# Queries' cast placed behind the exponentials, x of batch 0 loaded in its own steps, one transpose and one root moved ahead, in a post-norm transformer block on one core

## The chip, the cores and the metric

The kernel runs on one core of one Trainium2 chip. The metric is the device time of one execution in microseconds (us), lower is better. Times of separate runs and one profiled execution are given. All times inside the kernel are counted from the start of the profiled span.

## The reference

Input x has 4 batches of 512 tokens with 512 features, in float32. One block is computed: attention with 16 query heads of 32 and one shared key and value head, rotary position terms on queries and keys, a layer norm, a gated feed-forward with ternary weights, a layer norm.

```python
q = (x @ Wq + bq).reshape(B, T, H, HD).transpose(0, 2, 1, 3)
k = (x @ Wk + bk)[:, None]
v = (x @ Wv + bv)[:, None]
q, k = _rotary(q, HD), _rotary(k, HD)
attn = softmax(q @ k.T / sqrt(HD))
x = _layernorm(x + (attn @ v) @ Wo + bo)
quant = lambda w: clip(round(w / (mean(abs(w)) + 1e-8)), -1, 1)
hidden = sigmoid(x @ quant(w1).T) * (x @ quant(w2).T)
x = _layernorm(x + hidden @ quant(w3).T)
```

## The kernel before, in words

The attention is one list of 64 steps, `(b, c, t)`: 4 batches, 4 chunks `c` of four heads, 4 tiles `t` of 128 keys. A step computes transposed scores for four heads (`ps`, two PSUM tiles of two banks), exponentials on ScalarE (`es`, two instructions of 128x1024), and one step later the weighted values (`acc`). The maximum that softmax subtracts comes from a second product (`pmax`) made `LEAD` = 7 steps ahead and reduced on VectorE (`mx`). `ps` and `pmax` share the two buffers of the PSUM pool `ps_sc`, so a `pmax` waits until `es` has read the bank. In batch 0 the sums of the exponentials are a product (`den` from `es`); in batches 1 to 3 GpSimd adds them up over the four tiles (`total`, four instructions of 128x512 a step), and `den` is one product of `total` at the end of a chunk.

All engines but the DMA engines run their instructions in the order in which the program issues them: `act`, `dve`, `pool`, `mm`, `move` and `transpose` (lines 70 to 86) pin every instruction, so the trace shows L75 for all ScalarE, VectorE and GpSimd work, L80 for products, L83 for SP's transfers and L86 for transposes. The order is made by Python generators:

- `fill` hands out pieces of other work to TensorE between the steps: `project_in` (keys, values, queries of later batches), `project_out` (output product, first norm, transposes `pt`), `feed_forward`. Each `yield` gives the length of a piece.
- `late` is a list of generators with a slot number. `due()` (line 752) raises the slot and advances each one whose slot has come. It is called twice a step: in the middle, and at the end. So a small task such as `store_q` gets one piece of itself issued in each half-step.
- `quantized` is advanced by `quantize`, up to two jobs a step. A job loads one weight tile on GpSimd's queue four jobs ahead (`raw` from `in_wf`), takes its absolute sum (`junk`) or its sign (`sgn`) on ScalarE, finishes it on VectorE and stores it (`w` from `raw`).

`project_in` (line 262) makes one query chunk: product `pq`, then `turn` on VectorE (four instructions: `a`, a shuffle, a product, the addition that writes `q`), and then it enters `store_q` (line 328) in `late` with slot + 1, after the `yield` that follows. `store_q` casts `q` on ScalarE, subtracts on GpSimd to get the tail, and one half-step later stores `q` (`qw`) and head and tail (`qp`) through SP. `load_head` reads `qp` back (`qr`) for the `pmax` products. `load_xT` loads the transposed x of a later batch at the end of `project_in`, on SP's queue.

`normalize` (line 458) turns a chunk's sums into reciprocals through two small transfers (`flat`, `few`), spreads them (`rden`) and multiplies `ctxT` on GpSimd; the last chunk of a batch has fewer idle half-steps in it. `load_x` (line 525) loads four tiles of x of the same batch, and in the next four half-steps adds the output bias `bo_sb` to them on GpSimd; it is entered 6 slots after a batch's last step. `project_out` adds its product to these tiles, so they must be there by then.

After the last step two blocks are left: the rest of batch 2's feed-forward and batch 3's. `bank` (line 226) then hands out banks of `ps_mm` and `ps_sc` in turn. In the last part of a feed-forward, the `while` ahead of the products `po` holds them until enough tiles of the next batch are transposed (`transposed`); `split` copies each transposed tile as a head on ScalarE and a tail on VectorE (`y`). The first product `gu` of the next feed-forward needs all four tiles. At the very end, tiles 0 to 2 of batch 3 are normalized on ScalarE, and the last one by `last_norm` (line 676), half on ScalarE and half on VectorE.

Of the kernel before, what the change touches and what calls it, by code (L numbers as in the profile page):

```python
# [28 lines left out]
def postln_block(  # L29
# [232 lines left out]
    def project_in(b):  # L262

        s = batches[b]
        n = P - HD
        while now < NC * NT * (b - 2):
            yield 0

        pk = ps_mm.tile([P, T], F32, tag="mm", name="pk")
        for c in range(NC):  # L270
            mm(pk, wkv_sb[:, c, :], s.xT[c], c == 0, c == NC - 1)
            if c == 1:
                yield -1.8
        kv = work.tile([P, T], F32, tag="kv", name="kv", bufs=1)
        act.activation(kv[n:P], pk[n:P], AF.Identity, bias=bkv_sb[n:P, 0:1])
        s.kT = work.tile([P, T], F32, tag="kT", name="kT", bufs=3)
        rotation = turn(
            [(s.kT[0:n], slice(0, n)), (s.kT[n:P], slice(0, HD))],
            pk, bkv_sb[:, 0:1], bkv_sb[:, 1:2], n, now < 0,
        )  # L280
        next(rotation)
        yield 1.8
        next(rotation, None)
        if b > 0:
            late.append((slot + 2, split_k(b)))
        for c in range(NC):

            while b + 1 == B and c + 2 >= NC and not batches[0].projected:
                yield 0
            pq = ps_mm.tile([P, T], F32, tag="mm", name="pq")  # L290
            for d in range(NC):
                mm(pq, wq_sb[c][:, d, :], s.xT[d], d == 0, d == NC - 1)
                if d == 1:
                    yield -1.8
            if b == 0:

                if c == 0:
                    room = work.tile([P, NC, T], F32, tag="y0", name="room", bufs=1)
                q = s.q[c] = room[:, c, :]
            else:  # L300
                q = work.tile([P, T], F32, tag="q", name="q")
            rotation = turn(
                [(q, slice(0, P))], pq, bq_sb[:, c : c + 1], bq_sb[:, NC + c : NC + c + 1], P, now < 0
            )
            next(rotation)
            if c == 0:
                pv = ps_mm.tile([P, NT, HD], F32, tag="mm", name="pv")
                for t in range(NT):
                    transpose(pv[:, t, :], kv[n:P, ts(t, P)], ident[n:P, n:P])
                s.v = work.tile([P, NT, HD], F32, tag="v", name="v", bufs=3)  # L310
                act.copy(s.v, pv)
            yield 1.8
            next(rotation, None)
            if b > 0:
                late.append((slot + 1, store_q(b, c, q)))
            s.done = c + 1
        load_xT(NC if b == 0 else 2)
# [140 lines left out]
    def normalize(b, c):  # L458

        s = batches[b]  # L460
        if b > 0:
            s.den = ps_acc.tile([P, T], F32, tag="den", name="den")
            columns(s.den, ones[:, 0:HD], s.total, True, True)

        sums = work.tile([P, T], F32, tag="sums", name="sums", bufs=1)
        act.copy(sums, s.den)
        yield
        flat = [dram.tile([NG, T], F32, tag=f"flat{i}", name="flat", bufs=3) for i in range(2)]
        move(flat[0], sums.rearrange("(i r) k -> i r k", r=HD)[:, 0])
        yield  # L470
        few = small.tile([P, NG * T // P], F32, tag="few", name="few")
        move(few, flat[0].rearrange("i (r j) -> (i r) j", r=HD))
        yield

        if c + 1 < NC:
            yield
        dve.reciprocal(few, few)
        move(flat[1].rearrange("i (r j) -> (i r) j", r=HD), few)
        yield
        rden = work.tile([P, T], F32, tag="rden", name="rden", bufs=1)  # L480
        for i in range(NG):
            move(rden[ts(i, HD), :], flat[1][i].partition_broadcast(HD))
        yield
        if c + 1 < NC:
            yield
        pool.tensor_tensor(s.ctxT[c], s.ctxT[c], rden, ALU.mult)
        yield
# [94 lines left out]
    def feed_forward(b):  # L582
# [32 lines left out]
        for k, fs in enumerate(parts):  # L615
# [21 lines left out]
            ahead = NT // 2 if fs[-1] + 1 == NF else 1  # L637
            for some in [range(ahead)] + [(t,) for t in range(ahead, NT)]:

                while fs[-1] + 1 == NF and b + 1 < B and 0 <= batches[b + 1].transposed <= some[-1]:  # L640
                    yield 0
                pos = {t: bank("po") for t in some}
                last = len(fs) - 1
                early = [(t, n) for t in some for n in range(last)]

                put = len(early) - 1 if b + 1 == B and len(some) > 1 else len(early)
                for t, n in early[:put] + [(some[0], last)] + early[put:] + [(t, last) for t in some[1:]]:
                    for i in range(2):
                        mm(
                            pos[t],  # L650
                            h[n][i][:, ts(t, P)],
                            w3[k][n],
                            n == 0 and i == 0,
                            n == last and i == 1,
                        )
                for t in some:
                    dve.scalar_tensor_tensor(s.x[t], pos[t], 0.5, s.x[t], ALU.mult, ALU.add)
                    if fs[-1] + 1 < NF:
                        continue
                    stats(s.x[t], mv, t)  # L660
                    if b + 1 == B:
                        for done in range(max(t - 1, 0), t if t + 1 < NT else NT):
                            if done + 1 < NT:
                                for _ in layernorm(s.x[done : done + 1], mv[:, done : done + 1, :], True):
                                    pass
                                late.append((slot + 1, store(b, done)))
                            else:
                                last_norm(s.x[done], mv[:, done, :])
                    elif t == NT - 1:
                        late.append((slot + 1, layernorm(s.x, mv)))  # L670
                yield 0.24 * 2 * len(fs) * len(some)
# [1 line left out]
            for t in range(NT):  # L673
                late.append((slot + 6, store(b, t)))

    def last_norm(h, mv):

        y, shift = (small.tile([P, 1], F32, tag=f"end{k}", name="end") for k in range(2))
        act.activation(y, mv[:, 1:2], AF.Sqrt, bias=eps_t)
        dve.reciprocal(y, y)  # L680
        dve.scalar_tensor_tensor(shift, mv[:, 0:1], -1.0, y, ALU.mult, ALU.mult)
        left, right = slice(0, D // 2), slice(D // 2, D)
        act.activation(h[:, left], h[:, left], AF.Identity, bias=shift, scale=y)
        dve.tensor_scalar(h[:, right], h[:, right], y, shift, ALU.mult, ALU.add)
        pin(nc.scalar.dma_start(out=out[B - 1, ts(NT - 1, P), left], in_=h[:, left]))
        move(out[B - 1, ts(NT - 1, P), right], h[:, right])

    def store(b, t):
        move(out[b, ts(t, P), :], batches[b].x[t])
# [53 lines left out]
    PER = NC * NT  # L743
    LEAD = 7
    late = []
    slot = 0

    now = -1
# [3 lines left out]
    def due():  # L752

        nonlocal slot
        slot += 1
        for entry in list(late):
            if slot >= entry[0] and next(entry[1], "end") == "end":
                late.remove(entry)

    def ask(k):  # L760

# [6 lines left out]
    def find_maxima(k, *chunks):  # L768

        if k >= len(steps):  # L770
            return
        b, c, i = steps[k]
        if chunks[0] == 0:
            ask(k + HEADS)
            while batches[b].done <= c or (b and k not in heads):
                if batches[b].done <= c:
                    fill.one()
                else:
                    due()
                    ask(k)  # L780
        if b == 0:
            row_maxima(b, c, i, chunks[0] // 2)
        else:
            maximum(b, c, i, chunks, heads[k])
        if i == NG - 1 and chunks[-1] == NT - 1:

            late.insert(0, (slot + (1 if now < 0 else 2), spread(b, c)))
# [22 lines left out]
    for n, (b, c, t) in enumerate(steps):  # L810
# [7 lines left out]
        if last is not None and last[0] == 0:  # L818
            count(*last)
        last = (b, c, t, es)  # L820
        if t == NT - 1:
            begin = slot + 3
            late.append((begin, normalize(b, c)))
            if c == NC - 1:
                late.append((begin + 7, feed(b)))
                late.append((slot + 6, load_x(b)))
        if batches[-1].done < NC:

            find_maxima(n + LEAD, 0, 1)
            due()  # L830
            find_maxima(n + LEAD, 2, 3)
            quantize(1)
# [2 lines left out]
        else:  # L835
            find_maxima(n + LEAD, 0)
            fill.draw(0.4 * pace)
            find_maxima(n + LEAD, 1, 2)
            due()
            fill.draw(0.3 * pace, True)  # L840
            find_maxima(n + LEAD, 3)
# [72 lines left out]
```

## Time and profile before

| what | us |
|---|---|
| median of 3 runs | 693.89 |
| the runs | 690.67 to 695.45 |
| the profiled execution | 693.86 |
| its span, first to last instruction | 692.1 |
| ScalarE cast of the queries, 128x512 | 0.60 to 0.62 |
| GpSimd: tail of the queries, 128x512 | 1.26 to 1.33 |
| GpSimd: one step's `total`, four instructions | 4.94 to 4.97 |
| GpSimd: bias added to one tile of x | 1.26 to 1.28 |
| ScalarE: one step's `es`, two instructions | 1.93 to 1.94 |

The kernel's steps can be found in the trace by their `ps` products: those of batch 0 end at 154, the four of batch 1's first chunk start at 154.16, 162.32, 174.99 and 183.47. Batch 1's projection ran during batch 0, as did those of batches 2 and 3 in part. The attention ends at about 560; batch 2's last feed-forward products end at 622, and batch 3's feed-forward fills the rest.

A timeline row reads: start, duration, engine, line, operation, output from inputs, shape, number of instructions merged, and in brackets the engine's idle time before it and what ended it. PE is TensorE's product row, PEld its weight loads, DVE is VectorE, ACT ScalarE, POOL GpSimd, SP the queue that issues most transfers.

### The profile page before, as it was taken

The page shows a single profiled execution, that of the slowest core. Times are in us where ns is not written, and L with a number is a line of the kernel's source. Part 1 is how long each engine was busy: PE and PEld are TensorE (multiplying, and loading weights), DVE is VectorE, ACT ScalarE, POOL GpSimd, SP SyncE. Part 2 cuts the span into 40 slices and gives each one's busy share as a digit, 9 for nine tenths or more (in the row PEclk, how much of TensorE's full clock was granted, in tenths as well). Part 3 has the DMA queues.
Part 4 walks back from the last instruction along what each step waited for, and adds up shares of the span by engine and source line. Part 5 has one row for each costly group of instructions (what it writes and reads, how often), then busy time and mean ns, then how long its engine had stood idle before and what let it go on. Part 6 is the DMA issues. An engine that isn't in the chain of part 4 may idle for free.

```text
span 692.1 us, 9555 instructions
## 1 busy us (share of the span) xinstructions
PE 660.5 (95%) x3318; PEld 360.7 (52%) x3318; DVE 392.9 (57%) x570; ACT 290.3 (42%) x454; POOL 324.8 (47%) x414
## 2 busy tenths in 40 slices
PE   8989999998989979999999999999999999999995
PEld 6333333443333345565455565654554676777884
DVE  1887765785756655655555764455434433454435
ACT  2474556653443654434334445243344421234213
POOL 1624432446788684556555373666574803202000
PEclk9999999998999999999999999999999999999999
DMA  8746665787665465345223347341221464235631
GB/s 293 243 165 215 216 203 165 225 262 242 198 208 155 136 222 165 109 148 168 72 61 95 110 135 240 115 159 40 67 85 41 149 219 137 70 113 181 197 110 61
DMA packets 59807, 107.20 MB, mean 155 GB/s; under 512 B 13680, under 2 KB 14448, under 8 KB 59760
## 3 DMA queue, kind: packets, MB, share of 16 engines
q1 hardware_dynamic: 51696, 80.51, 37.6%
q0 software_dynamic: 7920, 25.96, 11.3%
q8 instruction: 26, 0.43, 0.2%
q14 instruction: 21, 0.17, 0.1%
q10 hardware_dynamic: 144, 0.13, 0.1%
HBM read 83.76 MB, written 22.81 MB: 154 GB/s over the span
## 4 chain that ended last, share of the span: by engine, by line
PE 85%; DVE 9%; ACT 3%; issue 1%; DMA 1%; POOL 0%; DVEq 0%; ACTq 0%; POOLq 0%
PE gu L80 24%; PE po L80 18%; PE ps L80 12%; PE pmax L80 9%; PE acc L80 8%; PE pq L80 7%; PE den L80 4%; DVE mx L75 3%; ACT es L75 2%; PE pk L80 2%; DVE xt L75 1%; PE warm L80 1%; DMA xT<-in_xT 1%; DVE y L75 1%; DVE st L75 1%
## 5 line engine op out<-in xcount | busy, mean ns | idle before, releaser
L75 DVE TENSOR_REDUCE mx<-pmax 128x1 f32<-128x512 f32 (+1 forms) x159 | 158.5, 1009 | 107.6 <-PE pmax L80 107.4
L75 ACT ACTIVATE es<-ps 128x1024 f32<-128x1024 f32 x128 | 124.2, 1022 | 126.9 <-PE ps L80 118.9
L80 PE MATMUL gu<-y,wg 128*128 128x512 f32 x704 | 173.7, 396 | 2.5 <-DVE y L75 1.6
L80 PEld LDWEIGHTS gu<-y,wg 128*128 128x128 f32 x704 | 130.9, 188 | 41.9 <-issue 6.9
L75 POOL TENSOR_TENSOR total<-total,es 128x512 f32<-128x512 f32 x96 | 123.6, 1318 | 50.6 <-ACT es L75 50.6
L80 PE MATMUL po<-wd,h 128*128 128x512 f32 x352 | 87.7, 396 | 3.7 <-DVE y L75 2.1
L75 POOL TENSOR_TENSOR total<-es 128x512 f32<-128x512 f32 x48 | 60.2, 1283 | 63.4 <-ACT es L75 63.4
L80 PE MATMUL pmax<-kr,qr 128*128 128x512 f32 x192 | 76.5, 463 | 8.8 <-ACT es L75 8.6
L80 PEld LDWEIGHTS po<-wd,h 128*128 128x128 f32 x352 | 64.7, 188 | 23.6 <-issue 3.4
L75 ACT CAST h<-hw 128x512 fp32r<-128x512 f32 x44 | 27.3, 620 | 97.6 <-DVE hw L75 97.5
L80 PE MATMUL acc<-es,v 128*32 128x512 f32 x512 | 68.2, 605 | 0.0
L80 PEld LDWEIGHTS pmax<-kr,qr 128*128 128x128 f32 x192 | 34.3, 192 | 63.3 <-ACT es L75 26.0
L75 DVE SCALAR_TENSOR_TENSOR hw<-th,gu 128x512 f32<-128x512 f32 x44 | 30.3, 688 | 57.5 <-PE gu L80 54.2
L75 DVE SCALAR_TENSOR_TENSOR xt<-po,xt 128x512 f32<-128x512 f32 x48 | 33.0, 688 | 47.8 <-PE po L80 47.6
L80 PE MATMUL po<-wo_sb,ctxT 128*128 128x512 f32 x128 | 59.1, 594 | 0.3 <-DVE hw L75 0.3
L80 PE MATMUL ps<-negm,ones_r 2*128 2x512 f32 x256 | 57.8, 788 | 0.0
L80 PE MATMUL ps<-qT,kT 32*128 32x512 f32 x384 | 55.2, 640 | 0.0
L75 DVE TENSOR_TENSOR h<-hw,h 128x512 fp32r<-128x512 f32 x44 | 41.3, 938 | 22.6 <-ACT h L75 22.3
L80 PE MATMUL pq<-xT,wq_sb 128*128 128x512 f32 x112 | 53.2, 603 | 1.0 <-ACT v L75 1.0
L75 POOL DMA_DIRECT2D raw<-in_wf x66 | 35.9, 546 | 37.5 <-ACT junk L75 19.3
L75 ACT ACTIVATE th<-gu 128x512 f32<-128x512 f32 x44 | 26.3, 598 | 47.5 <-PE gu L80 47.5
L80 PEld LDWEIGHTS po<-wo_sb,ctxT 128*128 128x128 f32 x128 | 23.9, 189 | 23.5 <-issue 21.1
(98 smaller groups left out, 624.6 us busy)
## 6 DMA issues: line engine op xcount, KB each, us to landing
wg<-w SPq DMA_DIRECT2D x88, 256.0 KB
raw<-in_wf POOLq DMA_DIRECT2D x66, 256.0 KB, 4.3
qr<-qp SPq DMA_DIRECT2D x96, 128.0 KB
wd<-w SPq DMA_DIRECT2D x44, 256.0 KB
w<-raw POOLq DMA_DIRECT2D x33, 256.0 KB, 4.3
qp<-q SPq DMA_DIRECT2D x48, 128.0 KB
rden<-flat SPq DMA_DIRECT2D x64, 64.0 KB
xt<-in_x SPq DMA_DIRECT2D x16, 256.0 KB
```

Of the source, the lines that this page charges most:

```text
L75: return lambda *args, **kw: pin(getattr(self.engine, name)(*args, **kw))
L80: pin(nc.tensor.matmul(out, lhsT=lhsT, rhs=rhs, start=start, stop=stop))
```

## The change

It has four parts.

1. In the main loop `project_in` asks at once whether `turn` is through; if so, `store_q` goes into a new list `middle`. `begin_middle()` moves that list into `late` just before the `due()` in a step's middle, so that the cast comes after that step's `es`.
2. `load_x(0)` is entered in the middle of batch 0 (step 8 of 16) instead of 6 slots after its last step; other batches keep their place.
3. The last chunk of batch 0 gets one more idle half-step in `normalize`, so that its `ctxT` product comes later in GpSimd's order.
4. After the last step, one more tile of the next batch must be transposed before the products `po` of a part's end. And the root of the last tile's norm is issued ahead of the norm of the tile before it; the last tile is normalized by VectorE alone, in two halves, each stored when done.

```diff
+            whole = b > 0 and next(rotation, "end") == "end" if now >= 0 else False
+            if whole:
+                middle.append((slot, store_q(b, c, q)))
             yield 1.8
             next(rotation, None)
-            if b > 0:
+            if b > 0 and not whole:
                 late.append((slot + 1, store_q(b, c, q)))
...
-        if c + 1 < NC:
+        if c + 1 < NC or b == 0:
             yield
         pool.tensor_tensor(s.ctxT[c], s.ctxT[c], rden, ALU.mult)
...
-                while fs[-1] + 1 == NF and b + 1 < B and 0 <= batches[b + 1].transposed <= some[-1]:
+                while fs[-1] + 1 == NF and b + 1 < B and 0 <= batches[b + 1].transposed <= min(
+                    some[-1] + (now == len(steps)), NT - 1
+                ):
                     yield 0
...
-                        for done in range(max(t - 1, 0), t if t + 1 < NT else NT):
-                            if done + 1 < NT:
-                                for _ in layernorm(s.x[done : done + 1], mv[:, done : done + 1, :], True):
-                                    pass
-                                late.append((slot + 1, store(b, done)))
-                            else:
-                                last_norm(s.x[done], mv[:, done, :])
+                        for done in range(max(t - 1, 0), t):
+                            norm = layernorm(s.x[done : done + 1], mv[:, done : done + 1, :], True)
+                            next(norm)
+                            if t + 1 == NT:
+                                end = last_scale(mv[:, t, :])
+                            for _ in norm:
+                                pass
+                            late.append((slot + 1, store(b, done)))
+                        if t + 1 == NT:
+                            last_norm(s.x[t], *end)
...
+    def last_scale(mv):
         y, shift = (small.tile([P, 1], F32, tag=f"end{k}", name="end") for k in range(2))
         act.activation(y, mv[:, 1:2], AF.Sqrt, bias=eps_t)
+        return y, shift, mv
+
+    def last_norm(h, y, shift, mv):
         dve.reciprocal(y, y)
         dve.scalar_tensor_tensor(shift, mv[:, 0:1], -1.0, y, ALU.mult, ALU.mult)
-        left, right = slice(0, D // 2), slice(D // 2, D)
-        act.activation(h[:, left], h[:, left], AF.Identity, bias=shift, scale=y)
-        dve.tensor_scalar(h[:, right], h[:, right], y, shift, ALU.mult, ALU.add)
-        pin(nc.scalar.dma_start(out=out[B - 1, ts(NT - 1, P), left], in_=h[:, left]))
-        move(out[B - 1, ts(NT - 1, P), right], h[:, right])
+        for k, engine in enumerate((nc.scalar, nc.sync)):
+            half = ts(k, D // 2)
+            dve.tensor_scalar(h[:, half], h[:, half], y, shift, ALU.mult, ALU.add)
+            pin(engine.dma_start(out=out[B - 1, ts(NT - 1, P), half], in_=h[:, half]))
...
+    def begin_middle():
+        late.extend(middle)
+        middle.clear()
...
+        if n == NC * NT // 2:
+            late.append((slot, load_x(0)))
         if t == NT - 1:
             begin = slot + 3
             late.append((begin, normalize(b, c)))
             if c == NC - 1:
                 late.append((begin + 7, feed(b)))
-                late.append((slot + 6, load_x(b)))
+                if b > 0:
+                    late.append((slot + 6, load_x(b)))
         if batches[-1].done < NC:
             find_maxima(n + LEAD, 0, 1)
+            begin_middle()
             due()
```

`begin_middle()` stands ahead of the other two calls of `due()` in a step's middle in the same way. In the order of instructions, TensorE's differs only in the place of one group of four transposes; ScalarE's and GpSimd's differ in the places of the casts and their tails, of the four bias additions and of one `ctxT`, and at the end; SP's in the places of `qw`, `qp`, the loads of x, and the `rows`, `qr`, `negm`, `rden` next to them.

## The prediction

> **What bounds the kernel.** I read the page first: its busy times, its slices, its chain.
>
> ```profile
> PE 660.5 (95%) x3318; PEld 360.7 (52%) x3318; DVE 392.9 (57%) x570; ACT 290.3 (42%) x454; POOL 324.8 (47%) x414
> PEclk9999999998999999999999999999999999999999
> ```
>
> TensorE is the bound nearly everywhere: 95% busy, and the chain is 85% PE. So a change pays only where PE stands still or runs slowly: 692.1 - 660.5 = 31.6 us of idle time, and wherever the granted clock is below 1. I then asked who PE waits for, and took the clock over short windows.
>
> ```profile
> PE pmax L80 <- ACT es L75: 9.5, 14, 2.6
> PE gu L80 <- DVE y L75: 1.6, 1, 1.6
> 163.10:166.50 3.40, 1.59 (x16) 1.00 0.82 298
> 166.50:169.90 3.40, 2.75 (x6) 0.50 0.88 251
> 169.90:173.30 3.40, 3.40 (x5) 0.50 0.87 259
> 173.30:176.70 3.40, 3.40 (x20) 0.99 0.64 172
> 190.40:193.80 3.40, 1.25 (x16) 1.00 0.81 242
> 193.80:197.20 3.40, 2.94 (x10) 0.50 0.60 183
> ```
>
> In the first two rows the numbers are us in total, times, longest. The other rows give the stretch, its length, PE's busy time, the granted clock, the DMA share and GB/s. Twice PE is busy for under half of a stretch (1.59 and 1.25 of 3.40 us) and the next one or two run at clock 0.50. So a wait is paid twice. The cause stands in the timeline, first of PE and ScalarE at 162 to 178, then at 189 to 198:
>
> ```profile
> 162.88 0.81 PE L80 MATMUL ps<-negm,ones_r 2*128 2x512 f32 x4
> 165.07 0.62 ACT L75 CAST q<-q 128x512 fp32r<-128x512 f32 x1 [5.74 <-DVE q L75]
> 165.59 1.93 ACT L75 ACTIVATE es<-ps 128x1024 f32<-128x1024 f32 x2
> 166.66 1.22 PE L80 MATMUL pmax<-kr,qr 128*128 128x512 f32 x2 [1.98 <-ACT es L75]
> 169.44 3.78 PE L80 MATMUL pk<-xT,wkv_sb 128*128 128x512 f32 x4 [0.49 <-DMA xT<-in_xT]
> ...
> 192.66 0.62 ACT L75 CAST q<-q 128x512 fp32r<-128x512 f32 x1 [5.22 <-DVE q L75]
> 193.19 1.93 ACT L75 ACTIVATE es<-ps 128x1024 f32<-128x1024 f32 x2
> 194.26 1.22 PE L80 MATMUL pmax<-kr,qr 128*128 128x512 f32 x2 [2.61 <-ACT es L75]
> 195.41 2.21 PE L80 MATMUL den<-total,ones 128*32 128x512 f32 x8
> ```
>
> The scores are ready at 163.69, but the exponentials (`es`) stand on ScalarE behind the queries' cast, and the cast waits for VectorE's `q`. `es` starts at 165.59, and PE's next product needs the bank that `es` reads.
>
> **The cast.** The changed program puts each cast just after the `es` of a step instead of before the next one; PE's order is unchanged there. Elsewhere PE's wait at this place is about 0.17 us.
> - First stall: 1.98 - 0.17 = 1.8 us. Its slow clock: two pairs of `pmax` at 1.22 and 1.20 against 0.73 make 1.0; `pk` at 3.78 against 1.98 makes 1.8; `pm` and the start of `pq` 0.2: together 3.0.
> - Second stall: 2.61 - 0.17 = 2.4. Its slow clock: `pmax` 1.22 against 0.73, `den` 2.21 against 1.07: 1.6.
> - Third place, batch 1 to 2: `pmax` waits 0.54 at 237.22 and 1.87 at 245.67 behind casts at 235.63 and 244.08; less 0.17 each, 2.1. The transposes behind wait 0.71 and 1.18 for VectorE's `y`, which hangs on ScalarE's casts behind the same `es`; I add 0.3. Bounds 1.4 (half of it returns in the transposes) and 3.5.
>
> What is late next? (a) The 0.49 before `pk` is a wait for xT, issued on SP at 163.50 and 5.90 us on the chain. At full clock and without the stall `pk` is due at about 166.5, so xT must be issued by about 160.6. SP held it behind the `qp` store, which waited for GpSimd's `q` (160.37), which stood behind `ctxT` (159.15, 3.77 waiting for its transfer). In the new order this `q` subtraction is two DMA pairs ahead of `ctxT`; its cast follows the `es` that end at 151.3, so it can run at about 152.3, `qp` issues behind `rden` (152.16 to 155.0) at about 156.7, and xT at about 159.6. So the 0.5 goes as well. (b) `den` needs GpSimd's sums: next part.
>
> **GpSimd's row.** Before: four additions of the output's bias (1.26 to 1.28 us each), `ctxT` (1.26) and casts' tails stand among the sums; the third `total` runs 190.97 to 195.92, while `den` starts at 195.41. It hid behind the stalls; with PE some 8 us earlier, `den` is due at about 187. After: from the first `es` (164.6), three `total` (4.94 + 4.97 + 4.95), one `q` 1.26, `kr` 1.28 and six DMA issues of 0.55 make 20.7, ending at 185.3: 1.7 us early. With two bias additions and `ctxT` still in front (3.8) it would be 189.1, 2 us late. So this edit earns nothing alone; it keeps the cast's gain. `ctxT`, one half-step later, then ends at 186.6; `po` wants it at about 189.
> The four loads of x (256 KB) are issued at about 105 instead of 178.24, 1.85 us of SP. Queued behind them on SP: `flat` (ready at 106.8), `qr`, `few`, `rows`, each with steps to spare. The additions wait on GpSimd for landings; the raw loads (`raw`, 103.73 and 110.69) queue behind the first two. A raw load lands in 4.3 to 4.8 us and its reader comes two steps (13 us) later in program order, so some 7 us of delay are hidden; price zero, bounds -0.5 and +3.
> Sum at 155 to 200: 1.8 + 3.0 + 0.5 + 2.4 + 1.6 = 9.3; bounds 5.5 and 10.5.
>
> **Three transposes ahead.** Only where batch 3 follows batch 2 after the attention. The `gu` at 622.01 runs one product and waits 1.59 for the last `y` (623.28 on VectorE), queued behind two pieces of `xt`, `st`, `mv`. In the new order the last transpose precedes the third `po`, and its `y` stands behind two such pieces instead of three, less one `y` moved ahead of them. By VectorE's rows (0.69 `y`, 0.69 `xt`, 0.69 `st`, 0.18 `mv`; about 1.6 a piece overlapped) the last `y` ends near 622.5 instead of 623.9: 1.4. A bank is reused sooner, so the second `po` may wait some 0.4 for the first `y`, which partly replaces the 0.38 at 617.55. I take 1.3, bounds 0.4 and 1.7.
>
> **The end.** Before, ScalarE does the norm of tile 2 (686.63, 0.81), then the root (687.35), and VectorE's two small steps end at 688.02; the halves run side by side to 688.65 and the store is issued at 688.68. After: root at 686.4, small steps end near 687.05, VectorE does both halves in turn (2 x 0.41) to 687.9. ScalarE still normalizes tile 2 until 687.5, then issues the left half; SP issues the right one at 687.9, tile 2 behind it. 688.65 - 687.9 is about 0.7; bounds 0.2 and 1.1.
>
> **Sum.** 9.3 + 2.4 + 1.3 + 0.7 = 13.7. The profiled execution took 693.86 (span 692.1), the median is 693.89, so nothing is to be corrected: 680.2 us. Bounds of the gains, 7.5 and 16.8, give 677.1 to 686.4.
>
> **Rivals.**
> *A: the slow clock stays.* By the trace, 1.8 idle us in one 3.4 us stretch cost the clock, 1.2 idle us (241.6 to 245.0, clock 1.00) did not. New waits of 1 to 2 us in these steps (VectorE is 29.2 of 45 us busy there) would keep the 3.0 + 1.6: 680.2 + 4.6 = 684.8. The Trainium skill, TensorE: Matmul & The Clock Gate, "Why this matters for your kernels", warns only of PE gaps over about 3 us; by that rule stalls of 1.98 and 2.61 would not have slowed the clock and removing them would not restore it, which gives this rival's time. The trace disagrees: 0.50 follows both. Chance 0.13.
> *B: another wait takes the place.* xT is issued as late as before, or GpSimd's sums still end after `den`. Then of the 9.3 only 3 to 4 remain, and the third place gives half: 693.9 - (3.5 + 1.2 + 1.3 + 0.7), 687.2, at worst 691. For it: GpSimd's slack is 1.7 us. Chance 0.11.
> *C: slower.* The x loads come 5 to 6 us later than I think, at 0.6 of the DMA engines busy there; GpSimd stands at the additions, raw loads miss their steps, and ScalarE waits for them ahead of `es`. It decides when the delay passes the 7 us of slack. Each late pair then stalls PE like the first stall, 1.98 + 3.0 = 5 us; with four such, 680.2 + 20 = 700. Against it: the queue held `ctxT` 6.77 us at 101.30 and nothing came of it. Chance 0.05.
> *The change does nothing:* excluded, its order differs where the stalls are.
>
> **Numbers.** Forecast 0.71, A 0.13, B 0.11, C 0.05. Runs of before spread from 690.67 to 695.45, so about 1% is what can be told. Faster by over 1% means below 687.0: forecast, A and a small part of B, 0.85; within 1%: most of B, 0.10; slower 0.05. The range takes the forecast's bounds, with 1 us for the spread, and A: 676 to 687.5.
>
> **What would show it.** PE's waits for `es` under 3 us in total; clock 1.00 from 6 us to the end of the products; `es` directly after its scores at each step; GpSimd's third `total` done before `den`; no bias additions after 130 us; xT issued before 161; `gu`'s wait for `y` under 0.8; the last normalize ending 0.7 us after the root's small steps. Wrong it is if a clock of 0.50 returns anywhere, or if `sgn` or `junk` wait for raw loads between 105 and 130.

## The result and the profile after

| | before | changed |
|---|---|---|
| median with the result | 692.47 us (6 runs) | 681.62 us (6 runs) |
| range | 690.67 to 695.45 | 680.24 to 685.92 |
| the profiled execution | 693.86 | 680.24 |
| its span | 692.1 | 678.5 |

The ratio is 0.9843, with a 95% interval from 0.9814 to 0.9873. Two more series of the changed kernel gave medians of 681.28 and 682.24 us; over all 17 runs of it the median is 681.77, over all 63 runs of the kernel before 692.56. So the change takes 10.8 us. The two profiled executions differ by 13.6 us, which is not the same thing; the reason is the clock, below.

The page's first lines, TensorE's busy time and its clock in 40 slices:

```profile
PE 655.9 (97%) x3318; PEld 358.2 (53%) x3318; DVE 390.2 (58%) x571; ACT 289.6 (43%) x453; POOL 324.9 (48%) x414
PEclk9999999999999999999999999999999999999998
```

PE is busy 4.6 us less with the same 3318 instructions: 0.7 of it in the warm-up products at the kernel's start, the rest because no product behind them runs at half clock in this execution. Its idle time fell from 31.6 to 22.6 us. Who PE waits for most (us in total, times, longest):

```profile
PE pmax L80 <- ACT es L75: 2.6, 10, 1.0
```

It was 9.5 us with a longest wait of 2.6. The wait of `gu` for `y` (1.6) has left the list. The timeline at the place of the two stalls, rows of all engines:

```profile
162.18 0.81 PE L80 MATMUL ps<-negm,ones_r 2*128 2x512 f32 x4
163.02 1.94 ACT L75 ACTIVATE es<-ps 128x1024 f32<-128x1024 f32 x2 [4.40 <-PE ps L80]
164.10 0.73 PE L80 MATMUL pmax<-kr,qr 128*128 128x512 f32 x2
165.15 0.61 ACT L75 CAST q<-q 128x512 fp32r<-128x512 f32 x1
166.08 1.98 PE L80 MATMUL pk<-xT,wkv_sb 128*128 128x512 f32 x4 [0.34 <-DMA xT<-in_xT]
...
180.83 4.96 POOL L75 TENSOR_TENSOR total<-total,es 128x512 f32<-128x512 f32 x4
185.44 1.94 ACT L75 ACTIVATE es<-ps 128x1024 f32<-128x1024 f32 x2 [2.74 <-PE ps L80]
185.76 1.27 POOL L75 TENSOR_TENSOR ctxT<-ctxT,rden 128x512 f32<-128x512 f32 x1
186.51 0.73 PE L80 MATMUL pmax<-kr,qr 128*128 128x512 f32 x2
187.17 1.07 PE L80 MATMUL den<-total,ones 128*32 128x512 f32 x8
```

`es` now starts 0.03 to 0.1 us after its scores end, the cast runs after it, and `pmax` takes 0.73 us instead of 1.22. GpSimd's third `total` ends at 185.79, `den` starts at 187.17 and takes 1.07 us instead of 2.21.

Aligned by the start of each step's scores, the two traces give the account (us gained so far, before minus changed). The 0.7 us up to batch 1's second step isn't the change's: it is won by 6.2 us, in the warm-up products, which start 0.213 us apart at first and 0.111 later, and go over to the short distance at about 6 us in the one execution and before 5 in the other. Without it the two profiles differ by 12.9 us.

| up to | before at | gained |
|---|---|---|
| batch 1's second step | 162.32 | 0.7 |
| the second step of its second chunk | 201.65 | 9.4 |
| the last step of its third chunk | 250.21 | 11.8 |
| the second step of its fourth chunk | 263.82 | 11.2 |
| the attention's last scores | 542.73 | 11.25 |
| the last tile's last addition | 684.72 | 12.8 |
| the last instruction | 692.1 | 13.6 |

### The profile page after: what moved, and what is told of

Its sections match the earlier page's. It is cut to its first block, busy times and chain, and to the rows that moved or that the text cites. A ratio compares the mean times of both kernels' runs of the same rounds, so it can differ in the third digit from the quotient of the medians.

```text
span 678.5 us, 9548 instructions
## 1 busy us (share of the span) xinstructions
PE 655.9 (97%) x3318; PEld 358.2 (53%) x3318; DVE 390.2 (58%) x571; ACT 289.6 (43%) x453; POOL 324.9 (48%) x414
## 4 chain that ended last, share of the span: by engine, by line
PE 83%; DVE 7%; ACT 3%; DMA 3%; issue 1%; SPq 1%; POOL 1%; DVEq 0%; ACTq 0%; POOLq 0%
PE gu L80 24%; PE po L80 19%; PE ps L80 11%; PE pmax L80 8%; PE acc L80 7%; PE pq L80 6%; PE den L80 3%; DVE mx L75 2%; ACT es L75 2%; DMA w<-raw 1%; PE pk L80 1%; DVE xt L75 1%; SPq L83 1%; PE warm L80 1%; DMA xT<-in_xT 1%
```

## The experiments

Runs of one series come from the same chip, with runs of the kernel before among them. `e1` to `e4` are one series (before: 693.14), `e5` to `e8` the second (before: 692.54), the last two the third (before: 691.71).

**The cast alone.** From the change only this is kept:

```diff
+            whole = b > 0 and next(rotation, "end") == "end" if now >= 0 else False
+            if whole:
+                middle.append((slot, store_q(b, c, q)))
```

> Only the cast's new place; the bias additions of batch 0 stay in batch 1's first steps and ctxT keeps its place on GpSimd. Theory (the row of GpSimd must be cleared for the cast's gain): the first stall and its slow clock go (5.3 us), so do 1.9 us at the third place, but at the second place den waits about 2 us for GpSimd's third total, because two bias additions and ctxT (3.8 us) stand ahead of it; the clock may fall once more there (1.6). Time against before: -7 to -9.5 us. Rival (GpSimd's row never mattered): -10.5 to -11 us, no wait of den for total, clock 1.00 throughout.

Measured: 693.45 us, ratio 1.0013 (0.9981 to 1.0046): nothing gained. The first stall is gone and the trace is 5.2 us ahead of before at the third and fourth step of batch 1, but 0.5 us two steps later. GpSimd's timeline, then PE's, then the clock over four stretches (length, PE busy, clock, DMA share, GB/s):

```profile
188.14 1.25 POOL L75 TENSOR_TENSOR ctxT<-ctxT,rden 128x512 f32<-128x512 f32 x1 [6.12 <-DMA rden<-flat]
189.36 1.25 POOL L75 TENSOR_TENSOR xt<-xt,bo_sb 128x512 f32<-128x512 f32 x1
190.58 4.92 POOL L75 TENSOR_TENSOR total<-total,es 128x512 f32<-128x512 f32 x4
```

```profile
191.89 5.24 PE L80 MATMUL den<-total,ones 128*32 128x512 f32 x8 [4.57 <-POOL total L75]
```

```profile
182.90:186.30 3.40, 3.40 (x24) 1.00 0.96 316
186.30:189.80 3.50, 0.92 (x6) 1.00 0.41 150
189.80:193.20 3.40, 1.31 (x3) 0.51 0.00 0
193.20:196.60 3.40, 3.40 (x7) 0.50 0.00 0
```

The theory named the right place, with too small a price. `den` waits 4.57 us, not 2, and the clock falls for 6.8 us. And it is not mainly work that stands ahead of `total`, but a wait: `ctxT` holds GpSimd for 6.12 us until `rden` has landed.

**GpSimd's row alone.** Only the early `load_x(0)` and the extra half-step of `ctxT`.

> Only GpSimd's row: x of batch 0 loaded in step 8 of batch 0 and ctxT one half-step later; the cast as before. Theory (the cast holds es, the row was hidden behind the stalls): both stalls of about 2 and 2.6 us and both stretches of clock 0.50 stay, -0.5 to +0.5 us. Rival (the bias additions on GpSimd were what held the chain): -4 to -9 us, and the second stall gone.

Measured: 692.06 us, ratio 1.0000 (0.9971 to 1.0029). Both stalls stay (1.34 and 2.58 us). The row alone is worth nothing that an interval of 2 us each way can show.

**Both, without the end's edits.**

> The cast's place and GpSimd's row together, the end of the kernel as before. The cast alone and the row alone were each worth nothing against before (1.0013 and 1.0000). Theory (the two need each other: the cast frees es, the row frees den): about -9 us, den without a wait for total, clock 1.00 through the attention. Rival (effects add up, the gain comes from the end's edits and the draw of the clock): 0 to -2 us.

Measured: 684.51 us, ratio 0.9892 (0.9861 to 0.9924), and `den` at 1.06 us without a wait. Nothing plus nothing makes 7.5 us: each edit removes one of two waits that end at about the same time, and the one left keeps the time.

**The end alone.** Only the transpose and the root.

> Only the two edits after the attention: one more tile transposed ahead and the root ahead of the norm. Theory: -2.0 to -2.4 us (1.3 to 1.6 for the transposes, 0.7 to 0.8 for the end), nothing moves before 600 us. Rival (the waits are only handed on to the next product): -0.8 us, the end alone.

Measured: 689.99 us, ratio 0.9974 (0.9945 to 1.0002). The size fits, the interval just takes in no change. In the traces with and without these edits (`e5` has none of them) the end is clearer: from the attention's last scores to the last instruction the changed kernel is 13.6 - 11.25 = 2.35 us shorter than before. The old end varies: from the last product's end to the last instruction it took 8.1 us in three of its five traces, 8.9 (`e5`) and 9.0 in the others; the new one took 7.3 in all seven.

**The stalls filled.** The kernel before, with extra products where PE stood still:

```diff
+        if n in (PER + 1, PER + 4):
+            busy = ps_acc.tile([P, T], F32, tag="den", name="busy")
+            for _ in range(3 if n == PER + 1 else 4):
+                mm(busy, ones, cos_sb, True, True)
```

> The kernel before with 3 and 4 extra products of ones and cos (result unused) on TensorE in the two places where it stood still for 2.0 and 2.6 us. Nothing else changes, the casts still hold es. Theory (the idle time in one stretch of 3.4 us is what halves the clock): the granted clock stays 1.00 there, the stalls' own 4.4 us stay (now partly busy), time -3.5 to -5 us. Rival (stalls under 3 us do not slow the clock, it falls for another reason): clock 0.50 stays, 0 to +1 us.

Measured: 690.90 us, ratio 0.9981 (0.9955 to 1.0006). The clock at the two places and at the third, which was not filled:

```profile
241.50:244.90 3.40, 1.51 (x8) 1.00 0.73 286
244.90:248.30 3.40, 2.64 (x12) 0.50 0.31 102
...
162.60:166.10 3.50, 3.50 (x24) 1.00 1.04 287
189.90:193.40 3.50, 3.50 (x13) 1.00 0.86 234
```

With the idle time filled the clock stays at 1.00 there, so idle time is what halves it. The ten runs bear this out: none has a mean clock under 0.993, while the 35 of the kernel before beside them go down to 0.983. The gain is smaller than expected, partly because the extra products run on when `es` has freed the bank: its first half ends at 166.04 and 191.82, and `pmax` starts at 166.83 and 192.35. At the second place the last piece of `den` also waits for `total` (193.50), so that only 0.6 us came instead of 1.6. And this execution lost 1.9 us where the clock fell at the third place, which it had not done in the profiled execution of before; by their mean clocks seven of the ten runs had no such loss. Those seven have a median of 690.5 us.

**One half of the row undone, twice.** The changed kernel with `ctxT` early again, and with x late again.

> The changed kernel with one thing undone: ctxT of batch 0's last chunk again one half-step earlier, ahead of the third total on GpSimd; x still loaded in batch 0. In the run with the cast alone ctxT waited 6.1 us for its transfer rden ahead of that total. Theory (this wait, not the bias additions, makes den late): den waits 3 to 4.6 us, the clock falls there, so +5 to +8 us against the changed kernel, near 687 to 690. Rival (the bias additions do it, as the prediction counted, 2 x 1.27 us): ctxT ahead costs 1.26 us less 1.7 us of slack, 0 to +0.5 us, near 681.5.

> The changed kernel with the other half undone: x of batch 0 loaded after batch 0 again and its bias added in batch 1's first steps, ctxT one half-step later as in the changed kernel. Theory (ctxT's wait is what mattered): total is late by the two additions, 2.5 us, less the slack, so den waits 0.5 to 1.5 us and the clock stays: +0.5 to +1.5 us against the changed kernel, near 682.5. Rival (the bias additions hold the row): den waits 3 us or more and the clock falls, +5 us or more, near 687.

Measured: `ctxT` early 683.65 us, x late 682.12, the changed kernel 681.28 in the same series. In the trace with `ctxT` early:

```profile
184.56 1.27 POOL L75 TENSOR_TENSOR ctxT<-ctxT,rden 128x512 f32<-128x512 f32 x1 [2.32 <-DMA rden<-flat]
185.78 4.98 POOL L75 TENSOR_TENSOR total<-total,es 128x512 f32<-128x512 f32 x4
```

and with x late:

```profile
184.05 4.98 POOL L75 TENSOR_TENSOR total<-total,es 128x512 f32<-128x512 f32 x4
189.37 1.27 POOL L75 TENSOR_TENSOR ctxT<-ctxT,rden 128x512 f32<-128x512 f32 x1 [0.34 <-DMA rden<-flat]
```

`ctxT` ahead costs 2.1 us in the steps around `den`, x late 1.1 (there `den` takes 2.17 us, spread out behind `total`). For `ctxT` neither expectation holds: its wait is 2.32 us, not 6.1, because SP's four loads of x no longer stand ahead of `rden`. From SP's last issue of `rden` to `ctxT`'s start it is 3.1 us here (181.47 to 184.56), and 5.6 and 5.7 where those loads stand ahead (182.56 to 188.14 with the cast alone, 183.64 to 189.37 with x late); the later issue makes up 1.1 of the difference, the longer transfer 2.5. So the two halves of the row help each other too. With both undone (the run with the cast alone), `den` waits 4.57 us and the clock falls; with one undone it is late by 1 to 2 us, which leaves PE busy enough. For x the first theory's size is right.

**The changed kernel again.**

> The changed kernel once more, for its spread. Theory (its stalls are too short to leave TensorE under half busy in any stretch of 3.4 us): clock at or above 0.995 in most runs and 680 to 683 us, against 689 to 698 for before, whose time follows its clock; a ratio of about 0.984. Rival (the first median was a lucky draw): median over 684.

Measured: 681.28 us, ratio 0.9846 (0.9819 to 0.9874). Two of six runs had a mean clock of 0.994. The profiled one of them shows a fall at the transposes in batch 1's third chunk:

```profile
236.10:239.50 3.40, 1.81 (x11) 0.99 0.94 278
239.50:242.90 3.40, 3.40 (x16) 0.50 0.97 284
242.90:246.30 3.40, 3.40 (x22) 1.00 0.43 140
```

Here too the stalls aren't short enough for every phase of the stretches. The prediction had named a clock of 0.50 anywhere as a sign of being wrong; by that sign it is wrong for this execution, at a place where it had counted on full clock.

**xT earlier.** The changed kernel, with the loads moved from the end of `project_in` to the place shown:

```diff
                 if d == 1:
+                    if b > 0 and c + 1 == NC:
+                        load_xT(2)
                     yield -1.8
```

> The changed kernel with the loads of xT for the last projection issued on SP as soon as the buffers' readers are issued, ahead of the queries' store instead of behind it. In the changed kernel pk still waited 0.34 us for it, in three of the other runs 0.78 to 1.07. Theory (a short wait that varies with the transfers): the wait is gone, -0.3 to -1.0 us against the changed kernel in the same call, near 680.8. Rival (the queries' store, now later by 1.1 us on SP, delays the next loads): 0 to +0.5 us.

> The changed kernel beside the one with xT early, on the same chip. Expected 680 to 683 us, as in its first two series (medians 681.62 and 681.28).

Measured: 681.36 us (0.9849 of before) beside 682.24 (0.9852). The wait of `pk` is gone and the steps behind it are 0.6 us ahead, but that execution lost 1 us to the clock at the transposes. By the ratios it is neither better nor worse.

## Why the prediction was right, point by point

**The cast and the two stalls: right.** Forecast 9.3 us at 155 to 200; the traces give 9.4 - 0.7 = 8.7. Of the signs named, `es` follows its scores, PE's waits for `es` are 2.6 us in total, and `pk` takes 1.98. At the first stall 4.6 came of the 5.3, for two reasons. xT, forecast to be issued before 161, came at 161.10: `qp` was issued earlier than forecast (155.05), but it and the loads `qr` behind it took 3.61 and 2.25 us on SP, and `pk` still waited 0.34. And the two pairs of `pmax` gave about 0.35 less than their rows promise, since the rows overlap in time: from the first pair's start until PE is through with the second it is 2.29 us before (166.66 to 168.95) and 1.64 after. The second stall gave 4.1, where 4.0 was forecast.

**What is late next: the place right, the cause and the price wrong.** The prediction says: "With two bias additions and `ctxT` still in front (3.8) it would be 189.1, 2 us late." It counted GpSimd's work and took `ctxT`'s transfer as landed. The run with the cast alone has `ctxT` standing 6.12 us for `rden`, `total` ending at 195.5 and `den` 4.57 us late, and then half clock for 6.8 us, so that the cast's gain is lost whole. Where `ctxT` is out of the way (x late), the counting holds: `total` ends at 189.03. That the row earns nothing alone is confirmed (1.0000).

**The x loads: right, with more delay than thought.** GpSimd's and SP's rows of the changed kernel:

```profile
107.21 2.42 SPq L83 DMA_DIRECT2D xt<-in_x  x4
112.07 2.52 POOL L75 TENSOR_TENSOR xt<-xt,bo_sb 128x512 f32<-128x512 f32 x2 [7.66 <-DMA xt<-in_x]
114.52 1.09 POOL L75 DMA_DIRECT2D raw<-in_wf  x2
```

They were issued 2 us later than forecast, GpSimd stood 7.66 us, and the raw loads went out at 114.5. ScalarE waits for no raw load, and PE has no new wait there: price zero, rival C did not occur.

**Third place: the size right, but a new wait behind it was overlooked.** Up to the last step of the third chunk the traces give 11.8 - 9.4 = 2.4, as forecast. The transposes' last wait (1.18) is unchanged, as it hangs on VectorE's order (`mx` and `few` ahead of `y`); the 0.3 came from the waits before it, since from the second group of transposes to the last it is 3.38 us before and 3.04 after. Then 0.5 is lost at the next product, the first `gu` of batch 0's feed-forward. Before, and in the third profile of the changed kernel, with SP's load of its weights:

```profile
241.29 1.40 SPq L83 DMA_DIRECT2D wg<-w  x3
253.32 2.00 PE L80 MATMUL gu<-y,wg 128*128 128x512 f32 x8
...
239.93 1.41 SPq L83 DMA_DIRECT2D wg<-w  x3
243.99 2.08 PE L80 MATMUL gu<-y,wg 128*128 128x512 f32 x8 [0.95 <-DMA wg<-w]
```

The load is issued 12 us ahead of its reader before, and 4 after. `gu` waits for it in four runs with the new cast (0.95, 0.86, 0.44 and 0.17 us). In the profile of the changed kernel the wait of 0.34 is put down to VectorE's `mx`; but before, `gu` starts while that `mx` still runs, so there too it is probably the load. Where the clock had fallen at the transposes, `gu` doesn't wait. No run here moves this load.

**Transposes and end: right.** 1.3 forecast, 1.6 measured (12.8 - 11.25, rounded); 0.7 forecast, 0.8 measured (1.6 against the longer old ends). The rows of the end:

```profile
673.58 0.29 ACT L75 ACTIVATE end<-mv,eps_t 128x1 f32<-128x1 f32 x1 [0.55 <-DVE ln L75]
673.82 0.81 ACT L75 ACTIVATE xt<-xt,ln 128x512 f32<-128x512 f32 x1
674.30 0.73 DVE L75 TENSOR_SCALAR xt<-xt,end 128x256 f32<-128x256 f32 x2
```

The root runs ahead of tile 2's norm, and both halves are done in 0.73 us on VectorE, which starts them while ScalarE still normalizes tile 2.

**The size of the whole: the step "so nothing is to be corrected" was wrong.** The sum, 13.7, is close to the difference of the two profiles (13.6), but that is partly luck: 0.7 of the 13.6 is the draw at the start, and the change's own part is 12.9. And the medians differ by only 10.8. The profiled execution of before had lost three stretches of 3.4 us to half clock; others lost none or more. Of the 57 runs of before whose clock is on record beside the experiments, the 20 with a mean clock of 0.995 or more have a median of 690.2 us, the 19 with less than 0.99 one of 693.7. The 14 runs of the changed kernel with 0.995 or more have 681.4. So at full clock the change is worth 8.8 us, and the sum's terms without the slow clock make 13.7 - 4.6 = 9.1: they hold. The terms of the slow clock, 3.0 + 1.6, are the ones that were too large. What its removal is worth is an average over phases, about 10.8 - 8.8 = 2.0 us, and the sum had taken it from one draw. The changed kernel loses some of it too (one of its first six runs had 0.989 and 685.92 us). The prediction's sentence that the clock would be 1.00 to the end holds for the profile of the changed kernel, not for every run.

**Rivals.** A, that the slow clock stays, did not happen at the two stalls. B happened in the run with the cast alone; in the change another wait took a place only at the third place, where `gu` waits for its weights. That the slow clock is of the stalls is shown by the run with extra products.

## What to carry to other kernels

When one wait is taken away, look up every wait that ends just behind it, and ask of each instruction ahead in that engine's queue not only how long it works but whether its input has landed: here two edits that were worth 0 each made 7.5 us together. An engine that runs in order should get the instruction that waits for a transfer as late as its reader allows. And compare kernels whose TensorE sometimes halves its clock by medians of many runs, or price the clock as an average over phases.

## What the runs showed of the hardware

The clock falls by stretches of 3.41 us. In the twelve profiles here, laid on the grid of their own clock events, a stretch in the attention and the feed-forward that ran at full clock with PE busy for 0.47 or less was followed by half clock in 8 cases of 8; at 0.60 or more never. Between 0.53 and 0.59 both occurred: it held in five, and fell in three, all at the transposes at 234 to 242. The busy share alone doesn't decide it, though: where the products end, one stretch at 0.45 (681.8 to 685.2, in the run with filled stalls) was followed by full clock. The way back goes by stretches too: a slow stretch with PE busy for 0.87 or more was followed by full clock in 11 cases of 11, one with 0.84 or less by a second slow one in 5 of 5. Since the grid isn't tied to the program (its first stretch at full clock starts anywhere from 4.6 to 7.4 us), the same stall of 1.9 us cost the clock in some executions (1.51 busy of 3.40, in the run with filled stalls) and not in others (2.21 and 2.02 of 3.40, in the profile of before).

The Trainium skill, TensorE: Matmul & The Clock Gate, "Why this matters for your kernels", says to avoid idle gaps of more than about 3 us between bursts of products. Here gaps of 1.9 to 2.6 us were enough, so on this point the measurement decides: what counted, with the exception above, was whether PE was busy for about half of such a stretch.
